# A conv and attention block on one core: slots of the tap tiles, the second pair's taps and the steps of the weight mixing

## The chip, the core and the metric

The kernel runs on one core of a Trainium2 chip. A core has TensorE (PE, matmuls into PSUM banks), VectorE (DVE), ScalarE (ACT), GpSimd (POOL) and SyncE (SP, whose queue issues nearly all of the DMAs). The metric is the device time of one execution in microseconds (us); lower is better. Everything is fp32.

## The reference

Sixteen images of 128 channels and 28 x 28 points (T = 784) go through four layers:

```python
x = x + L1conv(groupnorm(x), W)      # W: 128 filters, 128 channels, 3 x 3 taps
#   L1conv[f, t] = -sum over channels c and taps k of |W[f, c, k] - x[c, t shifted by k]|
x = quantized 3x3 conv, batch norm, clip, quantized 3x3 conv, batch norm, + x, quantized to 15 levels
t = tokens(x)                        # 784 tokens of 128
t = t + attention(ln(t))             # score[i, j] = v . tanh(Wi[i] + Wi[j]), softmax over j
t = t + two of 8 experts(ln(t))
t = t + linear_attention(ln(t))
t = t + spectral(ln(t))              # 16 filters phi, matrices mixed from 4 by softmax weights
```

The first layer is not a matmul: an absolute difference is needed for every filter, channel, tap and point. The scores need a tanh for every pair of tokens and channel.

## The kernel before, in words

**Taps.** The images are worked in eight pairs. For a filter f and a tap k a tap tile `d` of 128 channels x 1568 points (both images) is made in one of two ways: ScalarE writes |w - x| (kind "a", L1137), or VectorE writes max(w, x) (kind "m", L1139). As |w - x| = 2 max(w, x) - w - x, the sum of w is a constant per filter (`sw`), and the sum of x over channels comes from matmuls with ones on the padded input itself ("raw" taps, L1112, four matmuls each, with a filter mask of ones or zeros). A tile such as "m:13" holds two taps: VectorE writes the first, and a scalar_tensor_tensor (L1141) adds the max of the second.

**Sums.** The sum over channels is a matmul (L1126). The 128 filters are in four quarters of 32, and a step takes one tap tile of each quarter: 4 chunks x 4 quarters = 16 matmuls (32 records in the profile, two passes each), where the four quarters use four columns of 32 of the array side by side. They add into four PSUM banks `acc0` to `acc3`.

**Plans.** A `Plan` says for each filter which taps are made where. Pair 0 uses ALONE (four taps of a filter on ScalarE, for every fourth filter two), pair 1 SECOND (two on ScalarE, every fourth filter with nine tiles), the others BESIDE. A filter of ALONE or SECOND takes 8.25 tiles on average, so pairs 0 and 1 have 264 steps each; BESIDE has 208. `turns` starts each quarter at another tile, so that both kinds meet in a step.

**Slots.** Tap tiles lie in a ring of `RING` = 10 slots (`slot`), which also holds the loaded images and the convolutions' weights. A new tap tile waits until the matmuls that read the slot ten tiles before are done. Score rows have a pool of `ROWS` = 14 tiles of their own (128 x 394 each).

**What goes beside.** TensorE's instructions stand in the order in which the program writes them (the loop at L1154 to L1162 and `in_traced_order`, L156); the other engines' queues are ordered by the framework. Per step the program writes: score rows (`rows`), the taps of the next step, other engines' pieces of the lanes (`ahead`), the sums of this step, a raw tap, products of score rows, and TensorE's pieces of the lanes (`behind`). The lanes are generators that yield between pieces: `convs` (the quantized convolutions of the pair before, then the next pair's group norm), `conv_out` (spectral) and `chain`. The chain first prepares the weights, then does images one by one: `head`, `attend`, `experts`, `linear_attention`, `normed`. A lane moves on by its rate times `pace["by"]`, which is 208 over the steps of the pair, so that a pair gives the same number of turns whatever its steps. The chain's rate is `RATE_0` in pair 0.

**Preparation in pair 0.** `quantized_weights`, `token_constants` (32 bands: a matmul that flips, a copy on ScalarE, a store) and `spectral_weights` (35 matrices, each mixed from four by VectorE, L559 to L561; for an even and an odd one together 12 operations of 128 x 128 between two yields) use four spare parts of the score tile `sc` for what they load. At the end GpSimd fills `sc` with ones (L598).

**Scores.** In pair 0 there are none. In pair 1 the scores of image 0 can start when `head(0)` is done, which needs the convolutions of pair 0. A unit is four rows: four tanh on ScalarE (L727), then four matmuls side by side (L710). Scores of an image wait at their first block's end until the image before has been attended, as there is one `sc`. When the pairs are over, a last stretch does the rest with another form of the scores (L720, L722).

Of the kernel before, what the change touches and what calls it, by code (L numbers as in the profile page):

```python
# [16 lines left out]
T = HW * HW  # L17
# [6 lines left out]
class Plan:  # L24
# [2 lines left out]

    def __init__(self, kinds, classes, turns, maxima):  # L30
        self.kinds, self.classes, self.turns, self.maxima = kinds, classes, turns, maxima

    def streams(self):


        quarters = []
        for j, turn in enumerate(self.turns):
            mine = [(m, *x) for m in range(32) for x in self.classes[(m + j) % 4]]
            quarters.append(mine[turn:] + mine[:turn])
        return list(zip(*quarters))  # L40


def tiles(*taps):

    return [(kind, tuple(int(c) for c in s)) for kind, s in (x.split(":") for x in taps)]

ALONE = Plan(
    "alone", [tiles("a:0", "m:4", "a:2", "m:5", "a:6", "m:7", "a:8", "m:13")] * 3  # L50
    + [tiles("a:0", "m:4", "m:1", "a:2", "m:5", "m:3", "a:6", "m:7", "m:8")], (0, 2, 5, 7),
    [(1, "all"), (3, "all"), (4, "all"), (5, "all"), (7, "all"), (8, "fourth")])
MAXIMA = [(1, "all"), (3, "all"), (4, "all"), (5, "all"), (7, "all"), (8, "all"), (6, "all")]
SECOND = Plan(
    "beside", [tiles("m:13", "a:0", "m:4", "m:5", "m:6", "a:2", "m:7", "m:8")] * 3
    + [tiles("m:1", "a:0", "m:3", "m:4", "m:5", "a:2", "m:6", "m:7", "m:8")], (0, 2, 5, 7), MAXIMA)
BESIDE = Plan(
    "beside", [tiles("m:13", "a:0", "m:45", "m:6", "a:2", "m:78")] * 2
    + [tiles("m:13", "a:0", "m:7", "m:45", "a:2", "m:8", "m:6")] * 2, (0, 2, 4, 5), MAXIMA)
CONV_TAPS = [1, 2, 3, 4, 5, 6, 7]  # L60
MAGIC = 12582912.0
NLEV = 15.0
# [9 lines left out]
NE = 8  # L72
# [5 lines left out]
RING, ROWS = 10, 14  # L78


RATE_X, RATE_Y, RATE_S, RATE_C, RATE_A, RATE_0, RATE_T, RATE_Z = 1.2, 0.85, 2.0, 1.0, 1.5, 0.7, 2.0, 0.75


EV, PE = "other engines", "TensorE"
# [86 lines left out]
def kernel(ctx: ExitStack, tc: tile.TileContext, a: dict, out: bass.AP):  # L171
# [13 lines left out]
    NP = B // 2  # L185


    stage = {"pair": 0, "alone": False}
    turns = {"psx": 0, "psu": 0}

    def bank(pool, tag, more, name):
        turns[tag] = (turns[tag] + 1) % (1 + len(more)) if stage["alone"] else 0
# [80 lines left out]
    filters = {"all": ones, "fourth": fourth}  # L273

    sw = {}
    for plan in (ALONE, BESIDE):
        wsum = one.tile([P, P], F32, tag="gate", name=f"wsum_{plan.kinds}")
        part = one.tile([P, P], F32, tag="gt", name=f"part_{plan.kinds}")
        nc.vector.memset(wsum, 0.0)
        for k, of in plan.maxima:  # L280
            nc.vector.tensor_tensor(part, w0[:, k, :], filters[of], ALU.mult)
            nc.vector.tensor_tensor(wsum, wsum, part, ALU.add)
        q = ps("sw_ps")
        nc.tensor.matmul(q[:, :1], wsum, ones[:, :1], start=True, stop=True)
        sw[plan.kinds] = const.tile([P, 1], F32, name=f"sw_{plan.kinds}")
        nc.vector.tensor_copy(sw[plan.kinds], q[:, :1])
# [232 lines left out]
    def spectral_weights():  # L519


        yield EV
        lw = two.tile([P, NS], F32, tag="lw", name="lw")
        nc.sync.dma_start(lw, rows_of(a["L3_ffn_log_weights"], P))
        gu = two.tile([P, NS], F32, tag="gu", name="gu")
        nc.sync.dma_start(gu, rows_of(a["L3_ffn_gumbel"], P))
        sg = const.tile([P, NK], F32, name="sg")
        nc.sync.dma_start(sg, rows_of(a["L3_ffn_sigma"], P))
        quarter = const.tile([P, NK], F32, name="quarter")
        nc.vector.memset(quarter, 0.25)  # L530
# [12 lines left out]
        hard = const.tile([P, NS], F32, name="hard")  # L543
        nc.vector.tensor_reduce(s1, soft, AX.X, ALU.max)
        nc.vector.tensor_scalar(hard, soft, s1, None, ALU.is_equal)
        nc.vector.tensor_tensor(hard, hard, falling[:, :NS], ALU.mult)
        nc.vector.tensor_reduce(s1, hard, AX.X, ALU.max)
        nc.vector.tensor_scalar(hard, hard, s1, None, ALU.is_equal)
        w = const.tile([P, NS], F32, name="mix")
        nc.vector.tensor_tensor(w, hard, soft, ALU.subtract)  # L550
        nc.vector.tensor_tensor(w, w, soft, ALU.add)

        nc.vector.tensor_scalar(mask, ones[:, :1].to_broadcast([P, TH]), hard[:, 0:1], None, ALU.mult)
        for i in range(1, NS):
# [12 lines left out]
        def fetch():  # L567
            if sources:
                t = spare(NS * P).rearrange("p (s e) -> p s e", s=NS)
                nc.sync.dma_start(t, sources.pop(0).rearrange("s d e -> d s e"))  # L570
                loaded.append(t)

        for _ in range(3):
            fetch()
        yield EV
        for j in range(NAR):
            yield EV
            m = three.tile([P, P], F32, tag="mat", name=f"m_ar{j}")
            mixed(m, loaded.pop(0))
            fetch()  # L580
            nc.sync.dma_start(mats_ar[j], m)
        for k in range(NK):
            yield EV
            me = three.tile([P, P], F32, tag="mat", name=f"m_even{k}")
            mo = three.tile([P, P], F32, tag="mat", name=f"m_odd{k}")
            plus = loaded.pop(0)
            mixed(me, plus)
            mixed(mo, loaded.pop(0))
            dif = plus[:, 0]
            nc.vector.tensor_tensor(dif, me, mo, ALU.subtract)  # L590
            nc.vector.tensor_tensor(me, me, mo, ALU.add)
            nc.vector.tensor_scalar(me, me, sg[:, k : k + 1], None, ALU.mult)
            nc.vector.tensor_scalar(mo, dif, sg[:, k : k + 1], None, ALU.mult)
# [4 lines left out]
        nc.gpsimd.memset(sc, 1.0)  # L598
        yield EV


# [93 lines left out]
    def scores(b):  # L695
# [17 lines left out]
        for ib in range(NT):  # L713
            sp = pss.tile([P, 512], F32, tag="sp", name=f"sp{b}_{ib}")
            for m in range(Q):
# [6 lines left out]
                    nc.scalar.activation(th, th, AF.Tanh)  # L722
                    rows = [th[:, j, :] for j in range(4)]
                else:
                    rows = [rows_pool.tile([P, WIN], F32, tag="row", name=f"row{b}_{i + Q * j}") for j in range(4)]
                    for j in range(4):
                        nc.scalar.activation(rows[j], wi[:, i + Q * j : i + Q * j + WIN], AF.Tanh,  # L727
                                             bias=wi[:, i + Q * j : i + Q * j + 1])
# [245 lines left out]
    def spectral(b):  # L974
# [19 lines left out]
        for to in range(2):  # L994
# [15 lines left out]
            for n in [*mine, None]:  # L1010
# [88 lines left out]
    for p in range(NP):  # L1099
# [31 lines left out]
        def taps_of(n):  # L1131
            for j, (m, kind, taps) in enumerate(streams[n]):
                f = 32 * j + m
                d = slot(2 * T, f"d{p}_{f}_{taps[0]}").rearrange("p (h w) -> p h w", w=HW)
                k = taps[0]
                if kind == "a":
                    nc.scalar.activation(d, window(pad, k, 0, 2 * HW), AF.Abs, bias=w0[:, k, f : f + 1], scale=-1.0)  # L1137
# [77 lines left out]
```

## Time and profile before

| what | us |
|---|---|
| median of 3 runs (lowest, highest) | 12,013.93 (12,013.17, 12,015.77) |
| the profiled execution | 12,013.72 |
| its span | 12,012.0 |
| PE, DVE, ACT, POOL busy | 11,409.5, 10,731.9, 10,263.3, 186.2 |
| pair 0, first tap to the last sums | 31.3 to 914 |
| pair 1, to its last sums | to 2,153 |
| last x1p of pair 7 | 10,393 |

Engine names in the profile are PE, PEld (weight loads), DVE, ACT, POOL and SP. Line numbers are those of the kernel. A row such as `L1139 DVE TENSOR_SCALAR d<-pad,w 128x1568 f32 x562 | 555.8, 1041 | 70.7 <-PE acc L1126 70.6` says: 562 such instructions were busy for 555.8 us together, one took 1,041 ns on average, and the engine stood idle for 70.7 us just before them, of which 70.6 ended when the matmul of line 1126 was done. Durations of one engine overlap a little at their ends, so distances from start to start are shorter than mean durations. Where the line that ended a wait is "issue", nothing that the profile shows was waited for.

### The profile page before, as it was taken

Reading aid. Unit: us, or ns where it says so; the run is one execution under the profiler, and the core shown is the slowest. Engines: PE = TensorE matmul, PEld = TensorE weight load, DVE = VectorE, ACT = ScalarE, POOL = GpSimd, SP = SyncE. Lnnn points to the kernel's source line nnn. Section 1 sums busy time; section 2 is a strip of 40 time slices with the busy share of each in tenths; the row PEclk is TensorE's granted clock in tenths of the full one; section 3 lists DMA queues with packets and bytes.
Section 4 is the critical chain, followed back from the end, with each engine's and each line's share of the span. In section 5 each row is a group of like instructions: output and inputs, shape, how many; then the busy total and the mean of one; then the engine's idle time right before and its main releaser. Section 6 shows DMA issues by size and latency. Waiting matters only on the chain. (4 is left out here: it accounts for less than half of the span.)

```text
span 12012.0 us, 240466 instructions
## 1 busy us (share of the span) xinstructions
PE 11409.5 (95%) x99948; PEld 5214.0 (43%) x99948; DVE 10731.9 (89%) x15051; ACT 10263.3 (85%) x14568; POOL 186.2 (2%) x144
## 2 busy tenths in 40 slices
PE   8989999999999999999999999999999999999999
PEld 3333333444444444444444444444444444454446
DVE  9898789899999999899999999999999889988882
ACT  8884998979979899797998979889898898988882
POOL 0000000000000000000000000000000000000000
PEclk9999999999999999999999999999999999999999
DMA  0110000010110101001010110101110111011113
GB/s 24 58 32 5 1 1 6 17 34 27 33 32 18 35 28 32 24 28 33 26 38 17 31 33 25 31 26 31 34 31 19 29 31 34 27 54 51 54 54 97
DMA packets 376034, 372.49 MB, mean 31 GB/s; under 512 B 40296, under 2 KB 362144, under 8 KB 374944
## 3 DMA queue, kind: packets, MB, share of 16 engines
q1 hardware_dynamic: 374512, 355.35, 10.4%
q8 instruction: 787, 12.89, 0.4%
q14 instruction: 303, 2.48, 0.1%
q10 hardware_dynamic: 432, 1.77, 0.0%
HBM read 340.19 MB, written 16.78 MB: 30 GB/s over the span
## 5 line engine op out<-in xcount | busy, mean ns | idle before, releaser
L727 ACT ACTIVATE row<-wi 128x394 f32<-128x394 f32 x9904 | 5297.0, 625 | 254.1 <-PE sp L710 251.8
L1126 PE MATMUL acc<-d,sel_m 128*32 128x392 f32 x38656 | 5217.3, 502 | 144.2 <-DVE d L1141 133.3
L1139 DVE TENSOR_SCALAR d<-pad,w 128x1568 f32<-128x1568 f32 x4832 | 4783.5, 1031 | 456.9 <-PE acc L1126 454.3
L1126 PE MATMUL acc<-d,sel_a 128*32 128x392 f32 x18176 | 4502.8, 500 | 71.1 <-ACT d L1137 68.8
L1137 ACT ACTIVATE d<-pad,w 128x1568 f32<-128x1568 f32 x2272 | 3581.7, 1609 | 597.7 <-PE acc L1126 581.0
L1141 DVE SCALAR_TENSOR_TENSOR d<-pad,w,d 128x1568 f32<-128x1568 f32 x2112 | 3863.1, 1846 | 8.7
L1126 PEld LDWEIGHTS acc<-d,sel_m 128*32 128x32 f32 x38656 | 1714.0, 111 | 2121.2 <-issue 1653.9
L710 PE MATMUL sp<-row,vz 128*32 128x394 f32 x19808 | 2086.9, 495 | 1.1 <-ACT row L727 1.1
L1126 PEld LDWEIGHTS acc<-d,sel_a 128*32 128x32 f32 x18176 | 1349.4, 110 | 1111.1 <-issue 857.7
L1019 PE MATMUL u<-band,up 128*128 128x392 f32 (+3 forms) x8192 | 1752.9, 355 | 16.4 <-ACT us L1029 14.0
L1019 PEld LDWEIGHTS u<-band,up 128*128 128x128 f32 x8192 | 1330.0, 190 | 964.6 <-issue 281.2
L710 PEld LDWEIGHTS sp<-row,vz 128*32 128x32 f32 x19808 | 728.1, 110 | 1052.9 <-issue 791.1
L722 ACT ACTIVATE th<-th 128x1576 f32<-128x1576 f32 x660 | 969.8, 1521 | 118.4 <-DVE th L720 109.7
L720 DVE TENSOR_SCALAR th<-wi 128x394 f32<-128x394 f32 x2640 | 923.3, 420 | 12.0 <-PE sp L710 9.2
L1022 PE MATMUL out<-us,mat 128*128 128x392 f32 (+1 forms) x2048 | 923.6, 534 | 0.0
L1029 ACT COPY us<-u 128x392 f32<-128x392 f32 x1024 | 491.4, 480 | 480.6 <-PE u L1019 478.5
L710 PE MATMUL sp<-th,vz 128*32 128x394 f32 x5280 | 514.1, 503 | 47.7 <-ACT th L722 47.5
L884 DVE SCALAR_TENSOR_TENSOR t<-ex,gate,t 128x128 f32<-128x128 f32 x896 | 310.7, 347 | 83.9 <-PE ex L880 75.7
L1022 PEld LDWEIGHTS out<-us,mat 128*128 128x128 f32 x2048 | 311.7, 192 | 21.3 <-issue 8.3
L710 PEld LDWEIGHTS sp<-th,vz 128*32 128x32 f32 x5280 | 136.8, 109 | 340.7 <-issue 168.0
L880 PE MATMUL ex<-ew,xt 128*128 128x512 f32 x448 | 236.0, 609 | 37.1 <-DVE t L884 33.2
L795 PE MATMUL av<-vx,sc 128*128 128x129 f32 x1568 | 202.4, 282 | 37.3 <-DVE sc L784 18.7
(257 smaller groups left out, 4415.9 us busy)
## 6 DMA issues: line engine op xcount, KB each, us to landing
band<-band SPq DMA_DIRECT2D x1024, 196.0 KB, 2.4
mat<-mat SPq DMA_DIRECT2D x1024, 64.0 KB, 2.0
L_conv_w<-q_L_conv_w SPq DMA_DIRECT2D x16, 576.0 KB
ew<-in_L_ffn_expert_w_dram SPq DMA_DIRECT2D x16, 512.0 KB
eb<-eb_rows SPq DMA_DIRECT2D x16, 448.0 KB, 4.2
x<-in_x_dram SPq DMA_DIRECT2D x8, 784.0 KB
band<-band_out SPq DMA_DIRECT2D x32, 196.0 KB, 1.9
xr<-in_x_dram SPq DMA_DIRECT2D x8, 784.0 KB, 4.1
```

What stands on the lines that cost most here:

```text
L710: nc.tensor.matmul(sp[32 * j : 32 * j + 32, lo : lo + WIN], vz[:, 32 - m : 64 - m], rows[j], start=False, stop=m == Q - 1, skip_group_chec ...
L720: nc.vector.tensor_scalar(th[:, j, :], wi[:, i + Q * j : i + Q * j + WIN], wi[:, i + Q * j : i + Q * j + 1], None, ALU.add)
L722: nc.scalar.activation(th, th, AF.Tanh)
L727: nc.scalar.activation(rows[j], wi[:, i + Q * j : i + Q * j + WIN], AF.Tanh, bias=wi[:, i + Q * j : i + Q * j + 1])
L884: nc.vector.scalar_tensor_tensor(t[:, i, :], q[:, e * P : (e + 1) * P], gate[:, g : g + 1], t[:, i, :], ALU.mult, ALU.add)
L1019: nc.tensor.matmul(q[:, P * i : TH], up[:, to ^ odd, i, :], t[:, :w], start=i == 0, stop=i == 3)
L1022: nc.tensor.matmul(acc[:, lag:TH], m0, u[:, : TH - lag], start=False, stop=n is None and not copied)
L1029: nc.scalar.copy(u[:, :TH], q[:, :TH])
L1126: nc.tensor.matmul(accs[c][32 * j : 32 * j + 32, :NCK], sel[kind][:, 31 - m : 63 - m], d[:, 14 * c : 14 * c + 14, :], start=False, stop=n ...
L1137: nc.scalar.activation(d, window(pad, k, 0, 2 * HW), AF.Abs, bias=w0[:, k, f : f + 1], scale=-1.0)
L1139: nc.vector.tensor_scalar(d, window(pad, k, 0, 2 * HW), w0[:, k, f : f + 1], None, ALU.max)
L1141: nc.vector.scalar_tensor_tensor(d, window(pad, k, 0, 2 * HW), w0[:, k, f : f + 1], d, ALU.max, ALU.add)
```

## The change

It has four parts.

1. **Slots.** The pool of score rows becomes one constant tile `rows_in`, of 14 places that the program hands out in turn (`row`). In pair 0, when no rows exist, it serves as three more places for tap tiles; once `spectral_weights` is over (`stage["prepared"]`), the four spare parts of `sc` are four more. `tap_slot` goes round these places and the ten of the ring. The fill of `sc` with ones moves from the end of `spectral_weights` to the end of pair 0.
2. **SECOND.** The first six filters of each quarter (`EARLY`) use ALONE's tiles FOUR (four taps on ScalarE); the 26 others alternate TWO (two) and ONE (one). Every filter has 8 tiles: 256 steps. It gets its own `sw` and two more masks, `late` and `late_odd`; there are 8 raw taps instead of 7.
3. **Mixing.** `spectral_weights` yields after each of the two mixed matrices, and `RATE_0` goes from 0.7 to 0.9.
4. The masks lie in a tile that `head(0)` takes over later.

ALONE and BESIDE are written in another way, and their tiles stay as they are.

```diff
-    def __init__(self, kinds, classes, turns, maxima):
+    def __init__(self, kinds, tiles_of, turns, maxima):
...
-            mine = [(m, *x) for m in range(32) for x in self.classes[(m + j) % 4]]
+            mine = [(m, *x) for m in range(32) for x in self.tiles_of(m, j)]
...
-SECOND = Plan(
-    "beside", [tiles("m:13", "a:0", "m:4", "m:5", "m:6", "a:2", "m:7", "m:8")] * 3
-    + [tiles("m:1", "a:0", "m:3", "m:4", "m:5", "a:2", "m:6", "m:7", "m:8")], (0, 2, 5, 7), MAXIMA)
+FOUR, OTHER = tiles("a0 m4 a2 m5 a6 m7 a8 m13"), tiles("a0 m4 m1 a2 m5 m3 a6 m7 m8")
+ALONE = Plan("alone", lambda m, j: OTHER if (m + j) % 4 == 3 else FOUR, (0, 2, 5, 7), maxima("13457", fourth="8"))
+
+EARLY = 6
+TWO, ONE = tiles("m13 a0 m4 m5 m6 a2 m7 m8"), tiles("m13 a0 m4 m5 m6 m2 m7 m8")
+SECOND = Plan("second", lambda m, j: FOUR if m < EARLY else ONE if (m - EARLY) % 2 else TWO, (0, 2, 5, 7),
+              maxima("13457", late="68", late_odd="2"))
...
-RATE_X, RATE_Y, RATE_S, RATE_C, RATE_A, RATE_0, RATE_T, RATE_Z = 1.2, 0.85, 2.0, 1.0, 1.5, 0.7, 2.0, 0.75
+RATE_X, RATE_Y, RATE_S, RATE_C, RATE_A, RATE_0, RATE_T, RATE_Z = 1.2, 0.85, 2.0, 1.0, 1.5, 0.9, 2.0, 0.75
...
-    rows_pool = ctx.enter_context(tc.tile_pool(name="rows", bufs=ROWS))
...
+    rows_in = const.tile([P, ROWS * WIN], F32, name="rows_in")
+
+    def row(n):
+        k = turns["row"] = (turns["row"] + 1) % ROWS
+        return rows_in[:, WIN * k : WIN * k + n]
+
+    def tap_slot(name):
+        places = []
+        if stage["pair"] == 0:
+            places = [rows_in[:, 4 * WIN * k : 4 * WIN * k + 2 * T] for k in range(ROWS // 4)]
+            if stage["prepared"]:
+                places += [spare(2 * T) for _ in range(4)]
+        k = turns["tap"] = (turns["tap"] + 1) % (RING + len(places))
+        return places[k] if k < len(places) else slot(2 * T, name)
...
-    fourth = const.tile([P, P], F32, name="fourth")
-    nc.vector.memset(fourth, 0.0)
+    masks = one.tile([P, NE, P], F32, tag="dg", name="masks")
+    nc.vector.memset(masks[:, :3], 0.0)
+    fourth, late, late_odd = (masks[:, i, :] for i in range(3))
     for j in range(4):
         nc.vector.memset(fourth[:, 32 * j + 3 - j : 32 * j + 32 : 4], 1.0)
+        nc.vector.memset(late[:, 32 * j + EARLY : 32 * j + 32], 1.0)
+        nc.vector.memset(late_odd[:, 32 * j + EARLY + 1 : 32 * j + 32 : 2], 1.0)
...
-    for plan in (ALONE, BESIDE):
+    for plan in (ALONE, SECOND, BESIDE):
...
             mixed(me, plus)
+            yield EV
             mixed(mo, loaded.pop(0))
+            yield EV
...
-        nc.gpsimd.memset(sc, 1.0)
+        stage["prepared"] = True
...
-                    rows = [rows_pool.tile([P, WIN], F32, tag="row", name=f"row{b}_{i + Q * j}") for j in range(4)]
+                    rows = [row(WIN) for j in range(4)]
...
-                        u = rows_pool.tile([P, WIN], F32, tag="row", name=f"us{b}_{n}")
+                        u = row(TH)
...
-                d = slot(2 * T, f"d{p}_{f}_{taps[0]}").rearrange("p (h w) -> p h w", w=HW)
+                d = tap_slot(f"d{p}_{f}_{taps[0]}").rearrange("p (h w) -> p h w", w=HW)
...
+        if p == 0:
+            assert stage["prepared"]
+            nc.gpsimd.memset(sc, 1.0)
```

More of the change, by code (lines that the diff above doesn't have):

```diff
@@ L24 @@
 class Plan:
-    def __init__(self, kinds, classes, turns, maxima):
-        self.kinds, self.classes, self.turns, self.maxima = kinds, classes, turns, maxima
+    def __init__(self, kinds, tiles_of, turns, maxima):
+        self.kinds, self.tiles_of, self.turns, self.maxima = kinds, tiles_of, turns, maxima
     def streams(self):
@@ L37, in streams, with tiles, maxima @@
         for j, turn in enumerate(self.turns):
-            mine = [(m, *x) for m in range(32) for x in self.classes[(m + j) % 4]]
+            mine = [(m, *x) for m in range(32) for x in self.tiles_of(m, j)]
             quarters.append(mine[turn:] + mine[:turn])
         return list(zip(*quarters))
[L43 to L53, printed above, removed]
-SECOND = Plan(
-    "beside", [tiles("m:13", "a:0", "m:4", "m:5", "m:6", "a:2", "m:7", "m:8")] * 3
-    + [tiles("m:1", "a:0", "m:3", "m:4", "m:5", "a:2", "m:6", "m:7", "m:8")], (0, 2, 5, 7), MAXIMA)
-BESIDE = Plan(
-    "beside", [tiles("m:13", "a:0", "m:45", "m:6", "a:2", "m:78")] * 2
-    + [tiles("m:13", "a:0", "m:7", "m:45", "a:2", "m:8", "m:6")] * 2, (0, 2, 4, 5), MAXIMA)
+def tiles(taps):
+    return [(x[0], tuple(int(c) for c in x[1:])) for x in taps.split()]
+def maxima(all_, **some):
+    return [(int(k), "all") for k in all_] + [(int(k), of) for of, taps in some.items() for k in taps]
+FOUR, OTHER = tiles("a0 m4 a2 m5 a6 m7 a8 m13"), tiles("a0 m4 m1 a2 m5 m3 a6 m7 m8")
[4 more added lines that the diff above has]
+              maxima("13457", late="68", late_odd="2"))
+SIX, SEVEN = tiles("m13 a0 m45 m6 a2 m78"), tiles("m13 a0 m7 m45 a2 m8 m6")
+BESIDE = Plan("beside", lambda m, j: SEVEN if (m + j) % 4 > 1 else SIX, (0, 2, 4, 5), maxima("1345786"))
 CONV_TAPS = [1, 2, 3, 4, 5, 6, 7]
@@ L185 @@
     NP = B // 2
-    stage = {"pair": 0, "alone": False}
-    turns = {"psx": 0, "psu": 0}
+    stage = {"pair": 0, "prepared": False, "alone": False}
+    turns = {"psx": 0, "psu": 0, "row": 0, "tap": 0}
     def bank(pool, tag, more, name):
@@ L264 @@
         nc.vector.memset(t, 0.0)
-    fourth = const.tile([P, P], F32, name="fourth")
-    nc.vector.memset(fourth, 0.0)
+    masks = one.tile([P, NE, P], F32, tag="dg", name="masks")
+    nc.vector.memset(masks[:, :3], 0.0)
+    fourth, late, late_odd = (masks[:, i, :] for i in range(3))
     for j in range(4):
         nc.vector.memset(fourth[:, 32 * j + 3 - j : 32 * j + 32 : 4], 1.0)
-    filters = {"all": ones, "fourth": fourth}
+        nc.vector.memset(late[:, 32 * j + EARLY : 32 * j + 32], 1.0)
+        nc.vector.memset(late_odd[:, 32 * j + EARLY + 1 : 32 * j + 32 : 2], 1.0)
+    filters = {"all": ones, "fourth": fourth, "late": late, "late_odd": late_odd}
     sw = {}
-    for plan in (ALONE, BESIDE):
+    for plan in (ALONE, SECOND, BESIDE):
         wsum = one.tile([P, P], F32, tag="gate", name=f"wsum_{plan.kinds}")
```

## The prediction

> **What bounds the kernel now.** I read the page first (busy shares, forty slices), then busy times by stretch, then the groups of instructions inside each stage of the first two pairs, and the timeline where one number was needed. The profiled execution took 12,013.72 us with a span of 12,012.0; the median of the runs is 12,013.93. Sums below are against the span; add 2 for the median.
>
> ```profile
> PE   8989999999999999999999999999999999999999
> DVE  9898789899999999899999999999999889988882
> ACT  8884998979979899797998979889898898988882
> ```
>
> No engine is idle for long: three share the bound, and a shift of work pays only where the engine it relieves is the late one. The change works in pair 0 (31 to 917 us) and pair 1 (917 to 2154 us), so I asked for stretches there (busy us with counts: TensorE, weight loads, VectorE, ScalarE, GpSimd; then TensorE's clock):
>
> ```profile
> 200.00:300.00 100.00, 94.86 (x1092) 38.18 (x1087) 93.04 (x87) 93.41 (x62) 0.00 (x0) 1.00 0.01 2
> 600.00:700.00 100.00, 82.68 (x818) 29.43 (x810) 97.44 (x185) 68.09 (x45) 0.00 (x0) 0.97 0.23 65
> ...
> 1000.00:1100.00 100.00, 97.15 (x866) 36.94 (x863) 92.62 (x100) 40.35 (x29) 0.00 (x0) 1.00 0.02 7
> 1300.00:1400.00 100.00, 92.71 (x974) 41.00 (x970) 74.99 (x73) 100.00 (x158) 0.00 (x0) 1.00 0.00 1
> 1800.00:1900.00 100.00, 94.48 (x934) 41.48 (x930) 94.79 (x136) 75.03 (x103) 3.62 (x2) 0.98 0.05 15
> ```
>
> Pair 0 without preparation (first row) has all three engines at 93 to 95%. While weights are mixed (second) VectorE is the bound. Pair 1 starts with ScalarE at 40% and VectorE and TensorE full (third), then ScalarE is at 100% and VectorE at 75% (fourth), then, with attention of image 0 beside it, VectorE leads (fifth). The waits, by stage: 60 to 913 us, 917 to 1150, 1150 to 1750 (last column: idle before, and who ended it).
>
> ```profile
> L1137 ACT ACTIVATE d<-pad,w 128x1568 f32<-128x1568 f32 x468 | 714.3, 1604 | 102.7 <-PE acc L1126 101.2 <-DVE d L1139 1.4
> L1139 DVE TENSOR_SCALAR d<-pad,w 128x1568 f32<-128x1568 f32 x562 | 555.8, 1041 | 70.7 <-PE acc L1126 70.6
> ```
> ```profile
> L1139 DVE TENSOR_SCALAR d<-pad,w 128x1568 f32<-128x1568 f32 x163 | 158.9, 1031 | 28.6 <-PE acc L1126 28.6
> L1137 ACT ACTIVATE d<-pad,w 128x1568 f32<-128x1568 f32 x51 | 80.5, 1607 | 95.7 <-PE acc L1126 95.7
> ```
> ```profile
> L727 ACT ACTIVATE row<-wi 128x394 f32<-128x394 f32 x793 | 418.2, 622 | 0.1
> L1139 DVE TENSOR_SCALAR d<-pad,w 128x1568 f32<-128x1568 f32 x390 | 379.2, 1032 | 97.1 <-PE acc L1126 97.1
> L1137 ACT ACTIVATE d<-pad,w 128x1568 f32<-128x1568 f32 x124 | 195.9, 1606 | 0.7 <-PE acc L1126 0.7
> ```
>
> In pair 0 both tap engines wait for TensorE to give slots back (101 and 71 us). From 1150 to 1750 ScalarE never waits, and VectorE waits 97 us for it by way of TensorE.
>
> **Costs of one piece, start to start.** Mean durations overlap their neighbours, so I take distances from the timeline. 14 ScalarE taps in a row took 21.09 us: 1.51 each. VectorE taps in a row come every 0.95 us; a scalar_tensor_tensor tap takes 1.77 (717.72 to 719.49). TensorE's groups of four quarter matmuls start 0.33 us apart, two passes by four chunks: 8 x 0.33 = 2.62 us a step (a step is one tap tile in each quarter, 32 matmul records). From 1150 to 1750, 124 taps x 1.51 leave 413 us for 793 rows: 0.52 a row.
>
> **Part 1, deeper ring in pair 0.** The plan is unchanged: 264 steps. A FOUR filter costs VectorE 4 x 0.95 + 1.77 = 5.6 and ScalarE 4 x 1.51 = 6.0; an OTHER 5.7 and 4.5. Per step that is 2.70 for VectorE, 2.74 for ScalarE, 2.62 for TensorE. From 100 to 300 us there are 2,168 records, 67.75 steps, 2.95 us each: 7% above the floor. In the built program a tap's slot waits for the sums 2 or 3 steps back; after the change 3 or 4, and 4 or 5 once the preparation is over. The trace shows no deeper ring. Ends: nothing (the waits come from in-order syncs: a band copy on ScalarE waits for its matmul, 25 us in all) and all 71 us of VectorE's waits, since VectorE's own work, 264 x 2.70 + about 60 of mixing, sets the floor. I take half, 35: engines so close to balance lose time to unevenness of a step or so, which one more step of depth covers in part, and the lumps of mixing (12 small operations, 3.5 us) exceed a step of slack.
>
> **Part 2, mixing in finer steps, rate 0.7 to 0.9.** The same operations. Matmuls of bands move from steps 93-149 to 72-116, mixing on VectorE from steps 140-198 to 111-196. VectorE stays first there (2.70 + 0.7 a step against 2.74), so spreading saves only what lumps cost; that is inside the 35. SyncE's queue has the same fetches in the same order, a little earlier: 15 us of waits for these loads stay, between 0 and 15 saved; I take 0.
>
> **Part 3, the start.** One more plan's sum puts 8 product and add pairs on VectorE ahead of the first tap, 0.65 us a pair (19.85 to 20.50 and on): 5.2; masks 0.7. TensorE's matmul for the group means stands behind the new sum, so in the built order the second weight's quantizing (3.5 us) and the biases and near (2.3) now also go ahead of the padding, and GpSimd's rsqrt, for which the padding and every tap behind it wait, stands behind both weights' reductions and two powers. The first tap moves from 31.3 to about 43 us. The moved 5.8 us are gone from the first steps, where 31 to 100 us managed only 17 steps (4.0 each). Cost: +6 (0 to +12).
>
> **Part 4, the fill of sc.** GpSimd's memset moves from 706 us to the end of pair 0.
>
> ```profile
> 705.98 6.01 POOL L598 MEMSET sc<- 128x6272 f32 x1 [236.06 <-DVE m_odd L593]
> ```
> ```profile
> 705.70 9.96 DVE L1139 TENSOR_SCALAR d<-pad,w 128x1568 f32<-128x1568 f32 x5
> ```
>
> Five taps took 9.96 us instead of 4.8; the longest tap of the run is 6.18. The Trainium skill ("SBUF — State Buffer", the section on the two separate sides) says that GpSimd and a VectorE operation in a two-port mode exclude each other for a whole instruction. This speaks against the move: 5.1 us of VectorE are lost again where pair 1 starts, when no tap tile is in store. By the rule alone the loss only moves, and the sum is 11,943. By the rows, the first eight steps of pair 1 each carry four raw matmuls (2.9 us) beside their 2.6, so TensorE is behind anyway; I take 3 of 5 saved, which gives 11,940. Behind the memset on GpSimd stands only the rsqrt of image 0's first norm, wanted some 150 us later.
>
> Pair 0: -35 + 6 - 3 = -32 (0 to -70).
>
> **Part 5, the second pair's plan.** 264 steps become 256, an eighth raw tap adds 4 x 0.33 x 2 = 2.6 us of TensorE. Scores start at step 53 or 54 of the pair in both built programs, with 309 units of rows in pair 1 in both. I cost three stages, with 52, 129 and 83 steps now (1,664, 4,129 and 2,656 records), 50.5, 125 and 80.5 after.
>
> *Until scores start (233 us).* VectorE falls from 3.5 to 2.7 a step, ScalarE rises from 1.5 to 3.0. TensorE is next: 50.5 x 2.62 + 43 (convolutions) + 22 (raw) + 8 = 206. So at most 27. ScalarE also evicts the convolutions, in order behind more taps, and TensorE's next chunk waits for the one bank: 8 times up to 1.5 us. I take 15 (0 to 27).
>
> *Scores alone (600 us, ScalarE-bound).* Taps on ScalarE fall from 0.97 to 0.75 a step. Rows stay: 793 x 0.52 = 412. Taps 125 x 0.75 x 1.51 = 142. Sum 554, with 3 of eviction 557: -43. VectorE rises from 3.5 to 3.95 a step (7.4 for TWO, 8.4 for ONE), 125 x 3.95 = 494, 89% of 557; its 97 us of waiting are the cover. TensorE: 125 x 2.62 + 198 units x 0.66 + 15 = 473. If VectorE can't keep 89%, the gain falls to 20; end 50.
>
> *Scores beside attention (404 us).* VectorE now: 362 busy, 71 of it not taps. After: 80.5 x 3.95 + 71 = 389. No cover here: VectorE becomes first. It kept 97% from 600 to 700 and 95% from 1800 to 1900; at 92.5% it takes 420, +16 (+1 to +30).
>
> Pair 1: -15 - 43 + 16 = -42 (-10 to -75).
>
> **The rest.** Rows keep 14 places and wait 3 or 4 units back as before. Six units move from the end into pairs 2 and 4: 24 rows x 0.52 = 12 us more of ScalarE there, about as much less at the end; 0.
>
> Sum: 12,012 - 32 - 42 + 2 = 11,940 us.
>
> **Rivals.** (a) *All ring waits go.* Pair 0 falls to VectorE's floor (-62), pair 1 gains its good end (-70): 11,882. For it: 71 us of VectorE waits have one releaser. Against: TensorE's in-order stops remain. (b) *Depth is no cure.* The waits in pair 0 are syncs, the start costs 6 to 12, and only pair 1 gains: 11,975. For it: stalls at 740 to 750 us come from a small matmul waiting for VectorE, not from depth. (c) *Repaid:* the last stage of pair 1 takes back what the middle gives, pair 0 stands still: 12,005. (d) *Slower, by VectorE in pair 1.* From step 48 on VectorE must do 208 x 3.95 + 80 = 902 us in what are now 1,004. At 90% or more use, a gain; if the alternating plans starve TensorE of tiles on a ring of ten and use falls to 86%, it takes 1,049, +45, and with the start's 12 less 15 of the first stage 12,054. It decides at 902 / 1,004 = 90%. Against it: 95 to 97% was seen where VectorE was first. The change does what it says: the built order shows it, so no rival there.
>
> **Chances.** Forecast 0.45 (11,910 to 11,962), (a) 0.20, (b) 0.20, (c) 0.09, (d) 0.06. 0.2% is 24 us, about what a measurement can tell from no change: faster 0.85, same 0.09, slower 0.06. The range leaves out half of (a) below 11,880 and, above 11,995, (c) and (d) and a little of (b).
>
> **What would show it.** First tap near 43 us. The end of pair 0 (x1p on VectorE) near 885 instead of 914.6; waits of taps for TensorE in pair 0 down by half. One 6 us tap just after the pair's end instead of at 706. Pair 1 1,195 us long instead of 1,237, with ScalarE above 75% until scores start, still near 100% after, and VectorE above 88% there. Pairs 2 to 7 as long as before. It is wrong if ScalarE falls well below 100% in the middle stage (VectorE or the ring took over), or pair 0 ends after 905.

## Result, and the profile after

| what | before | after |
|---|---|---|
| median of 4 runs each (lowest, highest), us | 12,014.41 (12,013.17, 12,015.77) | 11,930.27 (11,921.62, 11,932.18) |
| the profiled execution; its span | 12,013.72; 12,012.0 | 11,928.61; 11,926.6 |
| first tap of pair 0 | 31.3 | 41.5 |
| end of pair 0 (first x1p on VectorE) | 914.6 | 864.0 |
| first score row | 1,151.4 | 1,105.3 |
| end of pair 1 | 2,153.6 | 2,072.4 |
| end of pair 1 to end of pair 7 | 8,237.0 | 8,231.2 |
| after that | 1,621.5 | 1,623.0 |

The ratio is 0.9928 (95% interval 0.9913 to 0.9943): 84 us less, where 74 were forecast. By the table, pair 0 gave 50.6 us (forecast 32), pair 1 gave 30.6 (forecast 42) and the rest 4 (forecast 0). The sum is near, though both of its main terms are off.

A gain of 0.7% can't be read from the page's forty slices, each 298 us wide. The stretches of the changed kernel show it (columns as before; those of pair 1 begin 50 to 90 us earlier, as its stages do):

```profile
600.00:700.00 100.00, 91.10 (x1000) 37.33 (x1000) 99.97 (x147) 83.68 (x56) 0.00 (x0) 0.97 0.14 40
...
1000.00:1100.00 100.00, 84.52 (x749) 30.68 (x748) 84.25 (x101) 60.05 (x44) 3.01 (x1) 0.93 0.00 1
1200.00:1300.00 100.00, 91.70 (x1038) 39.16 (x1034) 92.72 (x90) 100.00 (x163) 0.00 (x0) 1.00 0.01 2
1700.00:1800.00 100.00, 85.36 (x845) 36.79 (x841) 98.42 (x127) 64.53 (x97) 2.19 (x1) 0.97 0.05 15
```

While weights are mixed (first row), TensorE does 1,000 records in 100 us where it did 818, and VectorE has no gap left: 99.97%. In pair 1 ScalarE is at 100% beside 93% of VectorE (third row; before, 75%), and beside attention VectorE leads with 98%. The second row is the surprise: just before scores start, no engine is full.

The waits of the tap engines in pair 0 of the changed kernel, 60 to 862 us:

```profile
L1158 ACT ACTIVATE d<-pad,w 128x1568 f32<-128x1568 f32 x343 | 528.0, 1607 | 33.0 <-PE acc L1147 32.2 <-DVE stats L370 0.6
L1160 DVE TENSOR_SCALAR d<-pad,w 128x1568 f32<-128x1568 f32 x405 | 400.2, 1032 | 22.1 <-PE acc L1147 22.1
L1158 ACT ACTIVATE rows_in<-pad,w 128x1568 f32<-128x1568 f32 x101 | 159.8, 1606 | 36.6 <-PE acc L1147 36.3
L1160 DVE TENSOR_SCALAR rows_in<-pad,w 128x1568 f32<-128x1568 f32 x124 | 125.4, 1033 | 20.7 <-PE acc L1147 20.6
```

Tap tiles now go to ring slots (d), row places (rows_in) and the score tile. With 0.8 us more of VectorE's waits and 0.4 of ScalarE's in the last, VectorE's waits for TensorE fell from 70.6 to 43.5 us and ScalarE's from 101.2 to 68.9: by a third, not by half.

### The profile page after: what moved, and what is told of

Same layout as the page of the kernel before. It is cut to its first block, busy times and chain, and to the rows that moved or that the text cites. A ratio compares the mean times of both kernels' runs of the same rounds, so it can differ in the third digit from the quotient of the medians.

```text
span 11926.6 us, 239797 instructions
## 1 busy us (share of the span) xinstructions
PE 11351.0 (95%) x99702; PEld 5202.5 (44%) x99702; DVE 10750.4 (90%) x15057; ACT 10262.6 (86%) x14582; POOL 170.1 (1%) x144
## 4 chain that ended last, share of the span: by engine, by line
PE 59%; DVE 22%; ACT 16%; issue 3%; POOL 0%; DMA 0%; POOLq 0%; DVEq 0%; ACTq 0%; SPq 0%
PE acc L1147 24%; PE u L1040 11%; PE sp L731 10%; ACT rows_in L748 10%; DVE d L1160 8%; DVE d L1162 7%; PE out L1043 5%; ACT d L1158 5%; DVE th L741 2%; PE conv_ps L414 2%; PE ex L901 1%; PE acc L1133 1%; PE av L816 1%; DVE mx L792 1%; ACT th L743 1%
## 5 line engine op out<-in xcount | busy, mean ns | idle before, releaser
L748 ACT ACTIVATE rows_in<-wi 128x394 f32<-128x394 f32 x9928 | 5308.4, 627 | 296.2 <-PE sp L731 294.1
L1147 PE MATMUL acc<-d,sel_m 128*32 128x392 f32 x37136 | 5080.2, 503 | 112.0 <-DVE d L1162 105.2
L1160 DVE TENSOR_SCALAR d<-pad,w 128x1568 f32<-128x1568 f32 x4642 | 4594.8, 1030 | 353.3 <-PE acc L1147 350.0
L1158 ACT ACTIVATE d<-pad,w 128x1568 f32<-128x1568 f32 x2138 | 3385.5, 1612 | 471.6 <-PE acc L1147 468.1
L731 PE MATMUL sp<-rows_in,vz 128*32 128x394 f32 x19856 | 2074.2, 494 | 2.2 <-ACT rows_in L748 2.2
L731 PEld LDWEIGHTS sp<-rows_in,vz 128*32 128x32 f32 x19856 | 727.2, 110 | 1034.0 <-issue 800.0
L1043 PE MATMUL out<-us,mat 128*128 128x392 f32 (+1 forms) x1408 | 637.1, 534 | 0.0
L1050 ACT COPY us<-u 128x392 f32<-128x392 f32 x704 | 337.2, 479 | 175.8 <-PE u L1040 173.5
L1050 ACT COPY rows_in<-u 128x392 f32<-128x392 f32 x320 | 153.7, 480 | 301.6 <-PE u L1040 301.1
L1043 PE MATMUL out<-rows_in,mat 128*128 128x392 f32 (+1 forms) x640 | 286.4, 532 | 0.0
```

The source lines that it names most:

```text
L731: nc.tensor.matmul(sp[32 * j : 32 * j + 32, lo : lo + WIN], vz[:, 32 - m : 64 - m], rows[j], start=False, stop=m == Q - 1, skip_group_chec ...
L1043: nc.tensor.matmul(acc[:, lag:TH], m0, u[:, : TH - lag], start=False, stop=n is None and not copied)
L1147: nc.tensor.matmul(accs[c][32 * j : 32 * j + 32, :NCK], sel[kind][:, 31 - m : 63 - m], d[:, 14 * c : 14 * c + 14, :], start=False, stop=n ...
L1160: nc.vector.tensor_scalar(d, window(pad, k, 0, 2 * HW), w0[:, k, f : f + 1], None, ALU.max)
```

## Experiments: which part gives what

Each stage is read from the timeline of the profiled execution (us; a pair's end is its first x1p). `after`, e6, e8, e10 and e11 have the same pair 0 but for masks; it ended between 864.0 and 869.8, so a difference of less than about 6 us between two single profiles says nothing there.

| kernel | end of pair 0 | pair 1 until first row | pair 1 whole | pairs 2 to 7 | median |
|---|---|---|---|---|---|
| before | 914.6 | 236.8 | 1,239.0 | 8,237.0 | 12,014.41 |
| after | 864.0 | 241.3 | 1,208.4 | 8,231.2 | 11,930.27 |
| e1, slots alone | 863.4 | 236.1 | 1,238.4 | 8,247.0 | 11,973.17 |
| e2, second plan alone | 922.0 | 240.7 | 1,210.6 | 8,259.3 | 12,022.91 |
| e3, mixing alone | 911.9 | 233.7 | 1,240.6 | 8,232.0 | 12,011.50 |
| e4, slots and mixing | 854.9 | 231.9 | 1,238.2 | 8,230.9 | 11,956.83 |
| e5, e2 with another fraction | 923.1 | 240.7 | 1,210.7 | 8,233.9 | 11,991.77 |
| e6, seven early filters | 867.8 | 230.1 | 1,206.7 | 8,232.2 | 11,929.76 |
| e7, sums of the plans later | 862.8 | 247.3 | 1,214.4 | 8,234.7 | 11,933.32 |
| e8, plan by stage | 869.8 | 241.9 | 1,203.4 | 8,233.8 | 11,928.14 |
| e9, three more places only | 877.7 | 245.3 | 1,210.1 | 8,234.8 | 11,944.95 |
| e10, e6 and e8 together | 867.0 | 230.1 | 1,191.7 | 8,241.1 | 11,921.54 |
| e11, e8 with another fraction | 866.3 | 241.4 | 1,202.1 | 8,244.6 | 11,943.35 |

**e1: the slots alone.** The mixing and the second plan are those of before (here and below the diff is against the changed kernel, unless another is named):

```diff
             mixed(me, plus)
-            yield EV
             mixed(mo, loaded.pop(0))
-            yield EV
...
-RATE_X, RATE_Y, RATE_S, RATE_C, RATE_A, RATE_0, RATE_T, RATE_Z = 1.2, 0.85, 2.0, 1.0, 1.5, 0.9, 2.0, 0.75
+RATE_X, RATE_Y, RATE_S, RATE_C, RATE_A, RATE_0, RATE_T, RATE_Z = 1.2, 0.85, 2.0, 1.0, 1.5, 0.7, 2.0, 0.75
...
-    for plan in (ALONE, SECOND, BESIDE):
+    for plan in (ALONE, BESIDE):
...
-SECOND = Plan("second", lambda m, j: FOUR if m < EARLY else ONE if (m - EARLY) % 2 else TWO, (0, 2, 5, 7),
-              maxima("13457", late="68", late_odd="2"))
+NINE = tiles("m1 a0 m3 m4 m5 a2 m6 m7 m8")
+SECOND = Plan("beside", lambda m, j: NINE if (m + j) % 4 == 3 else TWO, (0, 2, 5, 7), maxima("1345786"))
```

> Only the slots (13, later 17 places for tap tiles in pair 0, sc filled at the pair's end); the second pair's plan, the mixing and the rate as before. Theory A, depth is what pair 0 lacked: x1p of pair 0 starts near 872 instead of 914.6 us, taps' waits for TensorE between 60 us and the pair's end fall from 71 (VectorE) and 101 (ScalarE) to about 45 and 70, and the time is 40 us below before, 11,974. Rival B, the lumps of mixing were the cause and depth alone does little: pair 0 ends after 900, time at most 15 us below before, 12,000.

Measured: 11,973.17 us, ratio 0.9964 (0.9951 to 0.9977), 43 us less, with pair 0 51 us shorter. The theory of depth holds. VectorE between 60 us and the end of pair 0, in before and then in e1: its busy time, and what it waited for most (us in total, times, longest):

```profile
60.00:913.00 853.00, 786.00 (x8366) 311.82 (x8354) 765.38 (x871) 725.12 (x500) 12.73 (x14) 0.99 0.11 33
...
DVE d L1139 <- PE acc L1126: 70.6, 78, 3.7
DVE m_ar L559 <- DMA sc<-in_L_ffn_M_u_dram: 4.3, 2, 3.8
DVE m_odd L559 <- DMA mat<-m_even: 3.7, 2, 2.9
DVE m_even L559 <- DMA band<-band: 2.4, 1, 2.4
```

```profile
60.00:862.00 802.00, 757.31 (x8381) 302.64 (x8376) 754.24 (x874) 722.59 (x501) 5.13 (x13) 0.99 0.12 34
...
DVE rows_in L1158 <- PE acc L1145: 24.8, 18, 4.1
DVE d L1158 <- PE acc L1145: 14.6, 12, 2.6
DVE sc L1158 <- PE acc L1145: 2.9, 2, 2.5
DVE m_ar L578 <- DMA mat_ar<-m_ar: 2.8, 1, 2.8
DVE m_odd L578 <- DMA mat<-m_even: 0.9, 3, 0.4
```

VectorE's waits for slots fell by 28 us (70.6 to 42.3), ScalarE's by 39 (101.2 to 62.2). VectorE's idle time fell by 40, from 87.6 (853 less 765.4 busy) to 47.8 (802 less 754.2): of the other 12, 7 are waits of the mixing for DMAs (11.2 to 4.0), and 3 are idle time before the mixing for which the profile shows no cause. VectorE's busy time fell by 11, of which 5 are the tap that the fill of the score tile had held.

**e2: the second plan alone.** Tap tiles of pair 0 have the ring only, the fill is back at the end of `spectral_weights`, and the mixing is as in e1. The score rows stay in `rows_in` here, as in every kernel from e1 to e11.

```diff
-        if stage["pair"] == 0:
-            places = [rows_in[:, 4 * WIN * k : 4 * WIN * k + 2 * T] for k in range(ROWS // 4)]
-            if stage["prepared"]:
-                places += [spare(2 * T) for _ in range(4)]
...
-        stage["prepared"] = True
+        nc.gpsimd.memset(sc, 1.0)
...
-        if p == 0:
-            assert stage["prepared"]
-            nc.gpsimd.memset(sc, 1.0)
```

> Only the second pair's plan with its own sum and masks; ring of 10, mixing and rate as before. Theory A: pair 0 ends 3 to 8 us later (the later first tap), pair 1 is 30 us shorter (1,209 instead of 1,239), all of it while scores run alone, time 25 us below before, 11,989. Rival B (the pairs lean on each other: pair 1 starts better because pair 0 ended with tiles in store): pair 1 less than 20 us shorter, time within 12 us of before.

Measured: 12,022.91 us, ratio 1.0006 (0.9997 to 1.0015). Pair 1 did what the theory said (28 us shorter), pair 0 took 7 us more for the later start, and yet nothing was left: pairs 2 to 7, whose plan is untouched, took 22 us more.

**e3: the mixing alone.** The two yields and `RATE_0` = 0.9 of the change; slots as in e2, the second plan as in e1.

> Only the finer steps of mixing and the rate 0.9; ring of 10 and second pair as before. Theory A (depth): pair 0 ends 5 to 12 us earlier, time 12,004 (-10). Rival B (lumps): pair 0 ends 25 us or more earlier, time 11,989 or less.

Measured: 12,011.50 us, ratio 0.9996 (0.9988 to 1.0005). Alone it does nothing that can be measured: pair 0 ended 2.7 us earlier, less than either theory had.

**e4: slots and mixing.** The changed kernel with the second plan as in e1.

> Slots and mixing together, without the second pair's plan. If the two parts add up, it is e1 + e3: theory A 11,964 (pair 0 ends near 862), rival B the same sum with the shares exchanged. If depth helps only where the steps are fine, it is faster than e1 + e3 by over 10 us.

Measured: 11,956.83 us, ratio 0.9952 (0.9935 to 0.9968). It saves 59 us, where e1 and e3 save 43 and 5, so by the number depth helps more where the steps are fine (12 us). In the profiles, beside deeper slots the finer steps take 8.5 us off pair 0 (863.4 to 854.9); 16 us lie in pairs 2 to 7, and the stretch after them gives 5 back. From e4 to the changed kernel, the second plan costs pair 0 9 us and takes 30 off pair 1.

The parts alone give spans of -41, +5 and -1 us, together -37; the whole gives -85. Of the 48 that are missing, 33 lie in pairs 2 to 7 (+10, +22 and -5 alone, -6 together), whose plan no part touches. (The slots part does move the score rows of these pairs into `rows_in`.)

**e5: why pairs 2 to 7 differ.** A lane adds rate times pace to its `due` and moves on by the whole part; the fraction stays. In the order in which the program writes its instructions, the lanes and the units of score rows stand at the same turn when pair 2 starts in before, e2 and the changed kernel; what differs is the chain's fraction: 0.818, 0.025 and 0.381. e5 is e2 with the last value set at the start of pair 2:

```diff
+        if p == 2:
+            due["units"], lanes[2].due = 0.0, 0.3813
```

> e2 (only the second pair's plan) with one difference: when pair 2 starts, the chain's fraction of a turn and the rows' are set to what they are in the changed kernel (0.3813 and 0 instead of 0.025 and 0). No work is added or taken away. Theory A, that e2 lost its gain to the turn in which each piece of the chain falls from pair 2 on: pairs 2 to 7 take 8,229 us as in the changed kernel instead of 8,257, and the time is 11,989 to 11,995. Rival: the plan itself slows what follows; then pairs 2 to 7 stay at 8,250 or more and the time at 12,017 or more.

Measured: 11,991.77 us, ratio 0.9979 (0.9971 to 0.9988), 31 us under e2. The stretch of pair 2 in e2 and then in e5, the same 1,368 us of time in both:

```profile
2132.00:3500.00 1368.00, 1313.30 (x11537) 595.05 (x11526) 1278.36 (x1480) 1202.61 (x1863) 18.15 (x10) 0.99 0.11 29
```

```profile
2132.00:3500.00 1368.00, 1316.53 (x11588) 597.08 (x11590) 1285.01 (x1494) 1210.53 (x1876) 18.60 (x10) 0.99 0.10 30
```

e5 does 14 VectorE and 13 ScalarE instructions more in the stretch, with every engine a little fuller (its 51 more matmul records are within what a trace can miss): the same instructions, interleaved otherwise. Pairs 2 to 7 took 25 us less. So e2's missing gain was lost to where pieces of the chain fall between steps.

## Experiments: the start of pair 1

The forecast gave the time until scores start 15 us less; it grew by 4.5. The waits of the tap engines there (864 to 1,105 us), and three stretches at its end:

```profile
L1158 ACT ACTIVATE d<-pad,w 128x1568 f32<-128x1568 f32 x95 | 146.2, 1603 | 47.2 <-PE acc L1147 47.2
L1160 DVE TENSOR_SCALAR d<-pad,w 128x1568 f32<-128x1568 f32 x112 | 113.5, 1057 | 52.5 <-PE acc L1147 52.1
```

```profile
866.00:1047.00 181.00, 177.38 (x1456) 71.31 (x1457) 127.06 (x125) 125.59 (x87) 5.33 (x1) 1.00 0.01 5
```

```profile
1047.00:1067.00 20.00, 13.13 (x119) 4.67 (x114) 16.95 (x26) 10.92 (x11) 0.00 (x0) 0.83 0.01 1
1067.00:1087.00 20.00, 15.34 (x150) 5.07 (x146) 18.63 (x28) 8.32 (x7) 3.01 (x1) 0.96 0.00 1
1087.00:1107.00 20.00, 17.50 (x149) 6.36 (x143) 18.93 (x19) 7.75 (x8) 0.00 (x0) 0.87 0.00 1
```

Until 1,047 us TensorE is busy for 177 of 181 us, VectorE for 127, and both tap engines wait for it. Then the first of the four quarters has used up its six early filters (their 48 tiles, less 7 that `turns` skips, are 41 steps), VectorE gets seven or eight of a filter's taps again and does the small operations of `head(0)` too: it is at 85 to 95%, and TensorE at 66 to 88%.

**e6: seven early filters.**

```diff
-EARLY = 6
+EARLY = 7
```

> The changed kernel with the first seven filters of each quarter, not six, made with four taps on ScalarE; the turns stay. Theory A, that VectorE is late in the last dozen steps before scores start: the stretch from pair 1's start to the first row falls from 239 to about 232 us, time 11,923. Rival, that the head's chain of small operations in TensorE's order sets that stretch: it stays within 3 us of 239.

Measured: 11,929.76 us, ratio 0.9928 (0.9913 to 0.9943). Until the first row, then the next stretch:

```profile
870.00:1098.00 228.00, 218.97 (x1842) 85.38 (x1844) 172.18 (x191) 163.65 (x118) 6.75 (x2) 1.00 0.01 4
1098.00:1665.00 567.00, 520.36 (x5698) 211.61 (x5690) 512.67 (x510) 560.89 (x908) 1.48 (x1) 0.98 0.01 1
```

The start shrank by 11 us, where the theory had 7 and the rival none, and TensorE was then busy for 219 of 228 us. But ScalarE is at 561 of 567 us next, and the taps given to it hold up the rows: first row to end of pair 1 took 9.5 us more. The whole took the same time, not the 7 us less of the theory.

**e7: the plans' sums later** (the weight sums of all three plans made by the chain inside pair 0, not ahead of the first tap).

```diff
-    for plan in (ALONE, SECOND, BESIDE):
+    def plan_sums(*plans):
+      for plan in plans:
+        yield EV
...
-    chain.add(quantized_weights(), token_constants(), spectral_weights(), head(0))
+    chain.add(quantized_weights(), plan_sums(ALONE, SECOND, BESIDE), token_constants(), spectral_weights(), head(0))
```

> The changed kernel with the three plans' weight sums made in pair 0 by the chain, in steps of two taps, not ahead of the first tap. Theory A, that their place ahead of the padding costs pair 0 its full length: first tap near 28 instead of 41.5 us, x1p of pair 0 near 852 instead of 864, time 11,918. Rival, that the work only moves: first tap earlier but pair 0 ends within 3 us of 864.

Measured: 11,933.32 us, ratio 0.9932 (0.9917 to 0.9947). The first tap came 13 us earlier, at 28.5, and pair 0 ended 1 us earlier, as the rival has it: the work only moves. That fits VectorE as the bound of pair 0, whose work costs the same wherever it stands; but in the changed kernel TensorE is as full there (763 us busy of 802, VectorE 759), so this cause is argued, not shown. Pair 1 took 6 us more; why stays open.

**e8: a plan by stage.** More ONE filters (one ScalarE tap) while ScalarE is full, TWO where attention stands beside.

```diff
-SECOND = Plan("second", lambda m, j: FOUR if m < EARLY else ONE if (m - EARLY) % 2 else TWO, (0, 2, 5, 7),
+SECOND = Plan("second", lambda m, j: FOUR if m < EARLY else ONE if m < 25 and (m - EARLY) % 3 else TWO, (0, 2, 5, 7),
...
-        nc.vector.memset(late_odd[:, 32 * j + EARLY + 1 : 32 * j + 32 : 2], 1.0)
+        for k in (1, 2):
+            nc.vector.memset(late_odd[:, 32 * j + EARLY + k : 32 * j + 25 : 3], 1.0)
```

> The changed kernel with the second pair's later filters placed by stage: filters 6 to 24 of a quarter two thirds with one tap on ScalarE (half before), 25 to 31 all with two. Theory A, ScalarE sets the middle stage and VectorE the last: pair 1 takes 1,190 instead of 1,208 us, time 11,912. Rival, with ten slots VectorE can't be kept over 90% busy beside ScalarE in the middle: pair 1 takes 1,205 us or more.

Measured: 11,928.14 us, ratio 0.9928 (0.9913 to 0.9943). Pair 1 took 1,203, not 1,190: nearer the rival's 1,205. Its stretches with scores alone and beside attention:

```profile
1111.00:1665.00 554.00, 512.04 (x5694) 212.66 (x5697) 517.93 (x523) 542.53 (x891) 2.20 (x1) 0.98 0.01 2
1665.00:2075.00 410.00, 370.09 (x3744) 149.78 (x3740) 362.81 (x534) 357.28 (x547) 6.16 (x4) 0.98 0.03 9
```

But VectorE is at 93% (518 of 554) in the first, so the rival's reason, that it can't be kept over 90%, is not what the trace shows. In the second VectorE had 363 us to do, 16 less than in the changed kernel, and the stage took 408 us as there (407): VectorE alone does not set it.

**e9: three more places only.**

```diff
-            if stage["prepared"]:
-                places += [spare(2 * T) for _ in range(4)]
```

> The changed kernel without the four places in the score tile: tap tiles of pair 0 have 13 places throughout, and not 17 once the weights are mixed. Theory A, that more depth goes on paying: in the profile of before, the stretch of pair 0 after 750 us did 1,098 records of sums in 100 us, and the changed slots with finer mixing did 1,170, which over the last 160 us of the pair is about 10 us, so pair 0 ends about 10 us later (near 874 instead of 864) and the whole takes about 11,940. Theory B, that three more places cure what depth can cure, and the faster rate after 750 us is theirs: pair 0 ends near 864 and the whole takes 11,930, within 4 us.

Measured: 11,944.95 us (11,933.86 to 11,947.57), ratio 0.9939 (0.9924 to 0.9954). Pair 0 ends at 877.7, and the five kernels with all places end it at 867.0 on average: 11 us for the four places in the score tile, as the theory that depth goes on paying has it. The other 40 or so of the slots' 51 us are then those of the three row places and of the moved fill, which no run parts.

**e10: e6 and e8 together** (both diffs).

> Two edits of the second pair together, each of which gave nothing alone: seven filters with four ScalarE taps instead of six, and of the later ones two in three with one ScalarE tap up to filter 24, then two taps each. Theory A, that they complete each other: the first takes 11 us off the time until scores start and put four ScalarE taps a quarter into a stage where ScalarE was full; the second takes ScalarE taps out of that stage. Then pair 1 takes about 1,194 us instead of 1,208, and the whole 11,917. Rival B, that VectorE can't be kept above about 93% of the pair beside ten slots, whichever way the taps are dealt: pair 1 takes 1,203 or more and the whole 11,926 to 11,931, a gain of less than 5 us over the change.

Measured: 11,921.54 us (11,916.77 to 11,924.45), ratio 0.9921 (0.9906 to 0.9936). Its stretches of pair 1, until scores start, scores alone, and beside attention:

```profile
870.00:1097.00 227.00, 217.97 (x1840) 84.91 (x1842) 171.16 (x188) 162.74 (x116) 5.95 (x2) 1.00 0.01 4
1097.00:1660.00 563.00, 523.50 (x5808) 214.82 (x5803) 529.95 (x537) 554.79 (x911) 1.48 (x1) 0.98 0.01 2
1660.00:2061.00 401.00, 364.53 (x3632) 148.90 (x3623) 351.84 (x515) 342.36 (x527) 6.16 (x4) 0.97 0.03 9
```

TensorE fills the first stage (96%) and ScalarE the second (99%), where VectorE stands at 94% (530 of 563) without holding it up; in the third no engine is above 91%. Pair 1 takes 1,191.7 us, 16.7 less than in the changed kernel, near theory A's 1,194. Rival B, with 1,203 us or more, falls. Pairs 2 to 7 took 10 us of it back, and the median is 9 us under the changed kernel, with intervals that overlap: better in pair 1, not shown to be better as a whole.

**e11: e8 with another fraction.**

```diff
+        if p == 2:
+            lanes[2].due = 0.65
```

> The stage-wise plan of the later filters, and at the start of pair 2 the chain's fraction of a turn set to 0.65 instead of 0.38; the work is the same. Theory A, that this fraction only has one bad place near zero (0.025 took 26 us more than 0.38, and 0.42 and 0.82 took no more than it): the whole is within 6 us of 11,928, and pairs 2 to 7 sum to 8,229 to 8,245. Rival B, that any fraction has a time of its own, scattered by some 20 us: the whole falls outside 11,920 to 11,936.

Measured: 11,943.35 us (11,937.58 to 11,945.59), ratio 0.994 (0.9924 to 0.9957). That is 15 us over e8 and outside theory A's bounds for the whole, as rival B has it. In the profiled runs, which are 6 us apart, pairs 2 to 7 took 11 us more than in e8 (8,244.6, just inside theory A's 8,245). So the place near zero is not the only bad one; that every fraction has a time of its own, one more value can't show. In the programs' written order the fraction is 0.381 or 0.418 in e3, e4, the changed kernel and e5 to e10, and all of these but e10 (8,241) stand at 8,231 to 8,235. The fraction alone doesn't settle it: before and e1 share 0.818 and differ by 10 us in these pairs. What e1 changes in these pairs is the place of the score rows alone, and no run tries that by itself.

## Why the prediction was right, and where it was off

The mechanisms named for pair 0 and for the scores alone held. That the sum came within 10 us is in part luck: pair 0 gave 19 us more than forecast and the rest 4 more, which made up for 11 less in pair 1.

**Part 1 and rival (b).** The mechanism held: e1 alone gives pair 0 51 us and the whole 43. The size was off. "I take half, 35" put half of VectorE's waits for slots; the runs show 28 of 71. But the forecast had only that wait in it. The mixing's waits for DMAs and its idle time without a shown cause, for which Part 2 put "between 0 and 15 saved; I take 0", gave about 10 us with the slots alone (14.2 to 4.0); why deeper slots help there was not tried. VectorE's busy time gave another 11, 5 of them the held tap of Part 4. The bound from both sides (0 to 71) was wide enough. Rival (a) fails, as 43 us of VectorE's waits for slots are left in the changed kernel; the forecast's own sign, waits down by half, did not come. (Every fourth filter of ALONE has three taps on ScalarE, `a0 a2 a6`, not two as the text on the plans says; the prediction's sums have three.)

**Part 2.** Right at 0 by itself (e3: -3 in pair 0), worth 8.5 us of pair 0 in e1 to e4, a little above the spread.

**Part 3.** First tap at 41.5 where about 43 was forecast; cost +6 forecast, 7 (e2 against before) and 9 (the changed kernel against e4) measured. e7 shows that the moment of the start is not what costs; VectorE's added work is the likely cause.

**Part 4.** Of VectorE's five us, the move saved two, not the three that were put; what that is worth in time no run shows, as none moves the fill alone. The timeline of the changed kernel at the end of pair 0:

```profile
864.00 2.73 DVE L1194 SCALAR_TENSOR_TENSOR x1p<-acc,sw_alone,xr 128x196 f32<-128x196 f32 x8
866.13 5.33 POOL L1190 MEMSET sc<- 128x6272 f32 x1 [148.76 <-DVE x1p L1194]
866.64 1.84 DVE L1162 SCALAR_TENSOR_TENSOR d<-pad,w,d 128x1568 f32<-128x1568 f32 x1
868.40 3.90 DVE L1160 TENSOR_SCALAR d<-pad,w 128x1568 f32<-128x1568 f32 x1
```

The held tap takes 3.90 us, 2.9 more than its 1.03, where before it lost 5.1. The reason given (TensorE is behind anyway) isn't what the rows show first: a scalar_tensor_tensor ran beside the fill at its usual 1.84 us, and only the tap behind it was held, until the fill was over at 871.46.

**Part 5, until scores start: the step that failed.** "TensorE is next: 50.5 x 2.62 + 43 (convolutions) + 22 (raw) + 8 = 206. So at most 27. ... I take 15." Measured: 4.5 us more. The sum took the stage as one, and its loads lie apart. All of the convolutions and raw taps fall into the first 181 us, where TensorE (177 busy) is late and VectorE's relief is worth nothing; the early filters end there, and in the last 58 us VectorE is late with what it always had. The rows of before said so already: TensorE at 97.15% from 1,000 to 1,100 us left little to gain from VectorE. ScalarE was to be above 75% here and was at 63% (151 of 239): of its 88 idle us, 47 were waits for slots and 41 for TensorE's other products. e6 supports the two bounds by taking 11 us off, and e10 repeats it (230.1 us in both).

**Part 5, scores alone.** 557 us and -43 forecast; 792 rows took 560 (1,105 to 1,665), so -40. VectorE 494 us busy forecast, 507 measured; ScalarE at 98% (551 of 560). Scores alone and beside attention, in before and then in the changed kernel:

```profile
1151.00:1751.00 600.00, 553.54 (x5785) 235.43 (x5781) 469.18 (x480) 597.77 (x926) 1.51 (x1) 1.00 0.01 1
1751.00:2154.00 403.00, 381.18 (x3879) 156.83 (x3875) 360.73 (x533) 368.06 (x563) 5.29 (x4) 0.98 0.03 9
```

```profile
1105.00:1665.00 560.00, 512.21 (x5650) 219.67 (x5646) 506.95 (x511) 550.97 (x892) 2.20 (x1) 0.99 0.01 1
1665.00:2075.00 410.00, 374.15 (x3799) 155.05 (x3791) 379.06 (x555) 343.69 (x546) 6.92 (x4) 0.98 0.03 9
```

**Beside attention.** +16 forecast, +5 measured (403 to 407): VectorE had 379 us to do, not 389, at the 92.5% use that was put. That VectorE is first here, as the forecast had it, is not confirmed: e8 took 16 us of it away and the stage took as long. Rival (d), VectorE at 86%, did not come; nor did rival (c), in which pair 0 stands still and the last stage takes back what the middle gives.

**The rest.** 0 forecast, -4 measured. That is less certain than it looks: e1, e2 and e11 show pairs 2 to 7 8 to 22 us longer than before with the same plan, so the 0 could have been off by as much. The range (11,880 to 11,995) covered that without having named it.

## What to carry to other kernels

Where engines are in balance, ask of each stage what the second bound is and when inside the stage each engine's load falls; a mean over the stage hides two bounds that follow each other. Storage that lies idle in a stage is worth using as buffers: seven more slots on ten, with the fill moved out of the pair, gave 51 us of 915, the last four of them still 11. And in an interleaved order, check the stages that an edit doesn't touch before judging it: the fraction of a turn carried over a boundary moved 8,235 us of work under an unchanged plan by up to 25, and hid a gain of 28.

## What the runs showed of the hardware

Whether a fill on GpSimd holds VectorE depends on VectorE's operation: beside the fill of 5.33 us the scalar_tensor_tensor with two tensor inputs kept its 1.84 us, and the one-input tensor_scalar behind it was held for 2.9 us. The profiles of e6, e8, e10 and e11 show the same two operations there, again with 1.84 and 3.90 us. The Trainium skill ("SBUF — State Buffer", the section on the two separate sides) has it so: an operation with two inputs in SBUF is kept out only by a GpSimd operation that reads SBUF, and a fill reads none.

At the start of pair 1 the granted clock of TensorE fell where TensorE was short of work, not where it was full: 0.83 to 0.96 in the three 20 us stretches with TensorE at 66 to 88%, and 1.00 in the 181 us before them at 98%. Over the span it is 0.990 before and 0.989 after.
